# A Restormer block on one core: a table moves single instructions along their engines, and a second replay hands out the buffers

## The chip, the cores and the metric

The kernel runs on one core of a Trainium2 chip. The metric is device time in microseconds of that core, from three runs of the kernel before: 3977.29, 3972.34 and 3972.2 us, median 3972.34 us. Shares and waits come from one profiled execution; a line number such as L1185 is a line of the kernel before, and in the changed kernel the same line of the function stands 590 lines further down (L1775).

## The reference

One transformer block over x of 16 x 128 x 96 x 96 (images, channels, rows, columns), all in fp32:

```
xn1 = layernorm(x over channels)
x   = x + attention(xn1)        # channel attention: 8 heads of 16 channels,
                                # q and k normalised over all 9216 pixels, softmax of a 16x16 matrix per head
xn2 = layernorm(x over channels)
h1  = w_in (512 x 128) @ xn2    # 1x1 convolution
h2  = depthwise 3x3 convolution of h1 (512 channels, zero padding)
x   = x + w_out (128 x 512) @ gelu(h2)
```

## The kernel before

An image's 96 rows are cut into 8 bands of 12 rows (`BR`), a band into 3 units of 4 rows (`UR`, 384 pixels); channels lie on the 128 partitions. The 512 hidden channels are 4 chunks of 128. Images overlap in time: while the bands of image i run through the convolutions, image i+1 goes through its first layernorm and its Gram matrix.

- **First norm (`norm`, second=False).** TensorE transposes 4 x 128 pixels (L872), ScalarE copies them out of PSUM (zT, L909), VectorE takes statistics (L880), GpSimd makes variance and its power -1/2 (ve_a, L885 and L889) and scales (L913), TensorE adds to the Gram matrix (g, L920) and transposes back (L968), ScalarE places the rows into the ring xn (L974).
- **Attention (`attention`)**, once an image: some 15 dependent steps that go from engine to engine, among them the product a on VectorE (L1112) and the TensorE product that reads it (L1116).
- **Second norm.** Mixing (L822, L831), the addition of x by an accumulating DMA that GpSimd issues (L834), transposes, statistics, variance and power (ve_b), transpose of the scales (L968) and the product into xn (VectorE, L972).
- **Depthwise convolution (`conv_job`)**, 467 jobs of one band and one chunk, spread over four engines. TensorE makes the hidden rows in 3 pieces (L1166), ScalarE copies each out of PSUM (L1171). Of the nine taps ScalarE multiplies two or three (pr, L1182). GpSimd adds the first of them to the middle tap (merged, L1185; at chunk 0 of a band that has a fourth such tap also L1188), and issues two accumulating DMAs: one product is added to another (pr<-pr, L1207), and that sum to the result (h<-pr, L1210). VectorE runs a chain of five taps or so: the **first tap** reads h1 and merged and writes the PSUM tile acc (L1194), middle taps add to acc (L1198), the last tap writes the result h3 (h<-h,ratio,acc, L1194). The second DMA lands on that result, and ScalarE's gelu (L1215) follows it.
- In some bands the fourth chunk's convolution is nine TensorE products (`by_matmuls`, L1278, gelu L1290 and L1292).
- **Output (`ffn_out`).** Four TensorE products per unit (L1314), VectorE adds to x (L1321), SyncE stores (L1325). SyncE also loads x (L799).

TensorE has four PSUM banks (h) for everything but the Gram matrix and acc. There are 8 pr, 8 h3 and 4 zT buffers, 5 and 2 buffers of x.

The order of the work isn't that of the loops. Each step is handed to the class `Plan` by `op` with its engine, a duration in ns, a place, its inputs and outputs; `order` (L283) plays these steps through once by events: when an engine is free it takes the ready step with the lowest place (a position with offsets from AT and SHIFTS). A step that needs a buffer takes one in that play. The order of the starts is the program, and every engine executes its own instructions strictly in that order. The durations are constants: a power on GpSimd 1020 ns (`T_POWER` = 360 + 165 x 4), a variance 190, an accumulating DMA's issue 890, a merge 2400. GpSimd and VectorE have one rule between them there: a GpSimd step that would begin while a first tap runs waits until that tap's end (L346).

```python
            elif engine == "POOL":
                rest = max(0, self.two - time) if k != self.ahead else 0
```

Of the kernel before, what the change touches and what calls it, by code (L numbers as in the profile page):

```python
# [46 lines left out]
ZT_BUFS = 4  # L47
BATCHES = 8
DIRECT = False
IN_TURN = ("zT", "tr", "h3", "pr", "xb", "x1")  # L50
AT = dict(
    load_w=-385.3, weights=-616.15, zeros=-141.7, load_a=-42.4, forth_a=-588.2, stats_a=1671.35, variance_a=269.75,
# [156 lines left out]
    31: dict(merge=3850.3, hidden=-0.2, kept=4295.2, products=1.1, tap=402.3, add_first=4907.6, gelu=-5949.9,  # L209
        conv=-11.3, conv_gelu=3477.9, out=2968.8, add=-5.3, store=-425.9),  # L210
}
STEP = dict(scaled=0.3, hidden=0.1, products=0.5, tap=0.166, conv=1.6, conv_tap=0.03, out=0.8, out_part=0.05)
SLACK = 150
LATE = 400
# [2 lines left out]
WAIT = dict(POOL=1090, SP=1300, ACT=1300)  # L217
# [19 lines left out]
class Plan:  # L237
# [6 lines left out]

    def __init__(self, **pools):
        self.free = {p: list(range(n)) for p, n in pools.items()}
        self.slot = {}
        self.ops, self.writer, self.readers, self.users = [], {}, {}, {}
        self.dma = 0.0
        self.two = self.held = self.lost = self.pool_free = 0.0  # L250
        self.ahead = None
# [31 lines left out]
    def order(self):  # L283
        ops, free = self.ops, self.free
# [5 lines left out]
        held = [[] for _ in ops]  # L290
        pending = {}
# [12 lines left out]
        events, starts, count = [], [None] * len(ops), 0  # L304
# [17 lines left out]
        def dispatch(engine, time):  # L322
# [13 lines left out]
            for t in o[5]:  # L336
                self.slot[t] = free[t[0]].pop(0)
                if t[0] in IN_TURN:
                    turn[t[0]].pop()
# [34 lines left out]
        while events:  # L374
            time, _, kind, what = heapq.heappop(events)
# [18 lines left out]
            if idle[what]:  # L394
                dispatch(what, time)
        assert None not in starts, "the buffers do not suffice"
        self.end = max(starts)
        return [ops[k][3] for k in sorted(range(len(ops)), key=lambda k: (starts[k], k))]


@with_exitstack
def tile_restormer_block(
# [175 lines left out]
    def t_dve(n):  # L578
        return 100 + 1.067 * n if n > 2 * UT else 67 + 1.05 * n
# [223 lines left out]
    def norm(i, second, place_of):  # L803
# [44 lines left out]
        def pixels(s, m):  # L848
# [11 lines left out]
            apart = i == 0 and not second  # L860
            from_psum = second or DIRECT or apart

# [90 lines left out]
        def zt_of(q):  # L953
            return ("h3", ("zT", q // 2), q % 2) if i == 0 and not second else ("zT", (name, q))
# [192 lines left out]
    def conv_job(j, g, n):  # L1147
# [115 lines left out]
    def by_matmuls(p, g, s):  # L1263
# [135 lines left out]
```

## Time and profile before

| | |
|---|---|
| time, median of 3 runs | 3972.34 us |
| profiled execution: span from the first to the last instruction | 3968.9 us |
| its time as a run | not listed; the median is 3.4 us above the span |
| busy: TensorE, VectorE, ScalarE, GpSimd | 3849.0, 3832.0, 3605.0, 3390.7 us |
| TensorE weight loads | 2482.4 us |
| DMA | 777.38 MB, mean 196 GB/s |
| granted TensorE clock | 0.997 |

Busy is the time in which an engine has an instruction under way, so the rest of the span is what it waited or had no work. TensorE and VectorE are both busy for 97% of the span; no single engine is the bound by a clear distance. What can change without any instruction changing is the idle time, and the views that show it are the busy time by stretches (500 us each, the columns are PE, PEld, DVE, ACT, POOL busy), the waits (engine, tile and line that waited, what ended the wait, us in total, times, longest) and the timeline (start, duration, engine, line, operation). PE is TensorE, DVE VectorE, ACT ScalarE, POOL GpSimd, SP SyncE.

### The profile page before, as it was taken

To read this page: it belongs to the slowest core of one execution; us is meant where nothing else is said; L and a number is where in the kernel's file an instruction comes from. 1 tells how busy PE (TensorE), PEld (TensorE's weight loads), DVE (VectorE), ACT (ScalarE), POOL (GpSimd) and SP (SyncE) were. 2 spreads that over 40 slices of the span, in tenths; PEclk is the share of its full clock that TensorE was granted. 3 is DMA by queue.
4 is the path that set the end of the run, shared out by engine and by line. 5 is a ranking of instruction groups with operands and counts; after the bars stand their busy time and mean duration, and the time that the engine had idled before them with its cause. 6 is when DMAs were issued, how large, how long until landed. Compare 5 with 4: busy or idle time off the path is not lost.

```text
span 3968.9 us, 50596 instructions
## 1 busy us (share of the span) xinstructions
PE 3849.0 (97%) x16467; PEld 2482.4 (63%) x16467; DVE 3832.0 (97%) x4392; ACT 3605.0 (91%) x5478; POOL 3390.7 (85%) x3107
## 2 busy tenths in 40 slices
PE   8999999999999999999999999999999999999999
PEld 7566666666666666666666666666666666666555
DVE  7999999999999999999999999999999999999998
ACT  3999899999899998999999999999999999999986
POOL 5998988888798898998889898888998888888674
PEclk9999999999999999999999999999999999999999
DMA  3999899999899999999999999999999999999996
GB/s 99 186 201 207 190 201 200 192 206 194 192 202 199 199 198 202 199 201 212 198 202 200 206 204 200 210 191 211 200 197 198 207 211 191 201 205 188 200 189 146
DMA packets 191689, 777.38 MB, mean 196 GB/s; under 512 B 22208, under 2 KB 23616, under 8 KB 191424
## 3 DMA queue, kind: packets, MB, share of 16 engines
q0 software_dynamic: 151920, 622.33, 82.7%
q1 hardware_dynamic: 38784, 151.75, 10.3%
q8 instruction: 129, 2.11, 0.2%
q14 instruction: 136, 1.11, 0.1%
q10 hardware_dynamic: 720, 0.07, 0.0%
HBM read 148.85 MB, written 75.50 MB: 57 GB/s over the span
## 4 chain that ended last, share of the span: by engine, by line
PE 24%; DVE 10%; ACT 5%; POOL 4%; DMA 4%; issue 3%; DVEq 0%; POOLq 0%; ACTq 0%
PE h L1314 7%; PE h L1166 6%; PE h L1278 6%; DVE acc L1198 5%; ACT pr L1182 2%; DMA pr<-pr 2%; DVE acc L1194 2%; DVE h L1194 2%; DMA h<-pr 2%; PE h L822 2%; PE h L968 1%; POOL merged L1185 1%; PE h L872 1%; PE g L920 1%; POOL merged L1188 1%
## 5 line engine op out<-in xcount | busy, mean ns | idle before, releaser
L1182 ACT ACTIVATE pr<-h,ratio 128x1152 f32<-128x1152 f32 x1494 | 1841.2, 1275 | 37.3 <-DMA pr<-pr 10.1
L1198 DVE SCALAR_TENSOR_TENSOR acc<-h,ratio,acc 128x1152 f32<-128x1152 f32 (+1 forms) x1308 | 1809.4, 1383 | 8.4
L1185 POOL TENSOR_TENSOR merged<-pr,h 128x1152 f32<-128x1152 f32 x466 | 1239.9, 2661 | 102.2 <-DVE acc L1194 48.5
L1166 PE MATMUL h<-xn,winT 128*128 128x384 f32 (+2 forms) x2802 | 1082.9, 495 | 17.8 <-ACT h L1171 6.1
L1314 PE MATMUL h<-h,woutT 128*128 128x384 f32 x3072 | 1079.4, 487 | 6.2 <-ACT h L1171 3.2
L1278 PE MATMUL h<-xn,comp 128*128 128x380 f32 (+2 forms) x2430 | 894.7, 483 | 7.6 <-ACT h L1171 4.0
L1314 PEld LDWEIGHTS h<-h,woutT 128*128 128x128 f32 x3072 | 567.9, 190 | 379.4 <-ACT h L1171 14.3
L1171 ACT COPY h<-h 128x384 f32<-128x384 f32 (+2 forms) x1401 | 653.2, 498 | 140.6 <-PE h L1166 137.4
L1194 DVE SCALAR_TENSOR_TENSOR acc<-h,ratio,merged 128x1152 f32<-128x1152 f32 x466 | 683.9, 1468 | 33.8 <-POOL merged L1188 13.9
L1166 PEld LDWEIGHTS h<-xn,winT 128*128 128x128 f32 x2802 | 499.0, 190 | 343.1 <-issue 34.9
L1210 POOL DMA_DIRECT2D h<-pr x466 | 476.2, 1022 | 236.6 <-DVE h L1194 54.6
L1215 ACT ACTIVATE h<-h,ksum 128x1152 f32<-128x1152 f32 (+1 forms) x586 | 616.9, 1085 | 53.7 <-DMA h<-pr 49.5
L1194 DVE SCALAR_TENSOR_TENSOR h<-h,ratio,acc 128x1152 f32<-128x1152 f32 x467 | 654.8, 1402 | 3.5
L1278 PEld LDWEIGHTS h<-xn,comp 128*128 128x128 f32 x2430 | 429.9, 190 | 237.9 <-issue 16.7
L1207 POOL DMA_DIRECT2D pr<-pr x466 | 487.4, 1059 | 73.8 <-ACT pr L1182 55.0
L889 POOL TENSOR_TENSOR ve_b<-ve_b,mhalf 128x4 f32<-128x4 f32 x288 | 377.8, 1325 | 7.9
L889 POOL TENSOR_TENSOR ve_a<-ve_a,mhalf 128x4 f32<-128x4 f32 x288 | 349.2, 1214 | 10.9
L913 POOL TENSOR_TENSOR zT<-zT,ve_a 128x512 f32<-128x512 f32 x270 | 348.2, 1295 | 6.4
L872 PE MATMUL h<-ident,x 128*128 128x128 f32 x2244 | 317.4, 275 | 18.3 <-ACT xn L974 4.6
L872 PEld LDWEIGHTS h<-ident,x 128*128 128x128 f32 x2244 | 262.3, 141 | 110.2 <-issue 37.9
L822 PE MATMUL h<-xn,mwT 128*128 128x384 f32 x768 | 289.9, 493 | 11.4 <-ACT x L831 6.5
L920 PEld LDWEIGHTS g<-zT 128*128 128x128 f32 x2160 | 270.2, 191 | 39.0 <-POOL zT L913 6.9
(187 smaller groups left out, 3923.2 us busy)
## 6 DMA issues: line engine op xcount, KB each, us to landing
pr<-pr POOLq DMA_DIRECT2D x466, 576.0 KB, 8.0
h<-pr POOLq DMA_DIRECT2D x466, 576.0 KB, 7.9
x<-in_x_dram SPq DMA_DIRECT2D x128, 576.0 KB, 7.5
out_dram<-x SPq DMA_DIRECT2D x127, 576.0 KB, 4.9
x<-in_x_dram POOLq DMA_DIRECT2D x123, 576.0 KB, 9.5
out_dram<-x SPq DMA_DIRECT2D x3, 192.0 KB, 1.9
h<-in_L_conv_w_in_dram SPq DMA_DIRECT2D x1, 256.0 KB, 4.4
h<-in_L_conv_w_out_dram SPq DMA_DIRECT2D x1, 256.0 KB, 4.5
```

Source lines behind the costliest of these rows:

```text
L872: nc.tensor.transpose(d["pT", q][:, k, :], xt[:, j * P : (j + 1) * P], ident)
L889: nc.gpsimd.tensor_tensor(rstd, rstd, mhalf, ALU.pow)
L1166: nc.tensor.matmul(rows(ph), lhsT=winT[:, n, :], rhs=window(xn, r0 + r, e - r, 1), start=True, stop=True)
L1171: nc.scalar.copy(window(h1_, r, e - r, 1), rows(d.pop(("ph", r))))
L1182: nc.scalar.activation(to, shifted(t), AF.Copy, scale=ratio[:, n, t : t + 1])
L1185: nc.gpsimd.tensor_tensor(merged, d["pr", dma_taps[0]], shifted(UNIT), ALU.add)
L1194: nc.vector.scalar_tensor_tensor(to, shifted(t), ratio[:, n, t : t + 1], also, ALU.mult, ALU.add)
L1198: nc.vector.scalar_tensor_tensor(to, shifted(t)[:, lo:hi, cut], ratio[:, n, t : t + 1], to, ALU.mult, ALU.add)
L1207: nc.gpsimd.dma_start(out=d["pr", dma_taps[1]], in_=d["pr", t], accum_op=ALU.add)
L1215: nc.scalar.activation(h3, h3, AF.Gelu, bias=ksum[:, z, n : n + 1])
L1278: nc.tensor.matmul(d["pc"][:, lo:hi, cut], lhsT=comp[:, t, :], rhs=window(xn, r0 + dy, UR, dx)[:, lo:hi, cut], start=(t == order[0]), stop ...
L1314: nc.tensor.matmul(rows(d["po"]), lhsT=woutT[:, n, :], rhs=h3s[g, n][:, s * UR : (s + 1) * UR, :], start=(k == 0), stop=(k == NCH - 1),)
```

## The change

No step, duration or place is altered, and both programs hold the same 10556 matmuls (as the program counts them), 4391 VectorE, 5451 ScalarE (and 32 table loads), 3103 GpSimd instructions and 264 SyncE DMAs. What is new comes after the play by events: its starts give a list of steps for each engine (and for each buffer pool that more than one engine takes from). `MOVES` then takes single steps out of such a list and puts them back some positions earlier (negative) or later: 1348 entries for PE, 790 for DVE, 2024 for ACT, 1050 for POOL, 13 for SP (all of them earlier, by 1 to 5), 27 for the pools h and h3. A second replay, `in_turn`, plays the moved lists strictly in order, and its choice of buffers and sequence is the program. Its waits are more detailed: a GpSimd DMA issue begins 480 ns after the end of a VectorE step that it needs, 240 after a ScalarE step; and a GpSimd step that is already running when a first tap begins ends 126 ns after that tap.

```diff
+MOVES = dict(
+    PE={6: -1, 11: -1, 13: -1, 18: 0, 19: -3, 26: -1, 28: -1, 29: 7, 33: -3, 37: 3, 38: 6, 39: -4, 47: -2, 48: -2,
...
+)
+ISSUE, FROM_POOL, PORT = dict(DMA=500, DVE=480, ACT=240), 170, 126
+PE_RATE, SPARE = 0.989, 75
...
-        return [ops[k][3] for k in sorted(range(len(ops)), key=lambda k: (starts[k], k))]
+        lists = {e: [] for e in ENGINES}
...
+        lists.update({p: ks for p, ks in takes.items() if len(takers[p]) > 1})
+        for name, ks in lists.items():
+            lists[name] = moved(ks, MOVES.get(name, {}))
+        return [ops[k][3] for k in self.in_turn(lists)]
...
+                if engine == "POOL" and ops[k][8]:
+                    from_ += ISSUE["DMA"] if ops[d][8] else ISSUE.get(of, 0)
+                elif of == "POOL" and engine == "DVE" and not ops[d][8]:
+                    from_ += FROM_POOL
...
+                    time = max(times[e], port) if ops[k][9] and last_two != e else times[e]
+                    if e == "POOL" and not ops[k][8]:
+                        time = max(time, taken)
...
+                if engine == "DVE":
+                    taken, at = time + ns, free_at["POOL"]
+                    if last_pool is not None and not ops[last_pool][9] and time < at < taken + PORT:
+                        by = taken + PORT - at
+                        free_at["POOL"] += by
...
+def moved(ks, moves):
+    rest = [k for n, k in enumerate(ks) if n not in moves]
+    for n, by in sorted(moves.items(), key=lambda m: m[0] + m[1]):
+        rest.insert(n + by, ks[n])
+    return rest
```

Three places show what the moves are like; the prediction calls them A, B and C.

**Place A, GpSimd, image 8, band 5 (about 2212 to 2218 us of the profile).** Before, the merge for chunk 2 (L1185 reading h_2) stands behind the variance and power of group 15, the addition of x, an accumulating DMA and the variance of group 16:

```order
L885 TENSOR_SCALAR ve_b_15_14692<-st_b_15_14667 128x4
L834 DMA x_9_0_14654<-in_x_dram 128x1152
L1207 DMA pr_148<-pr_145 128x1152
L889 TENSOR_TENSOR ve_b_15_14692<-ve_b_15_14692,mhalf 128x4
L885 TENSOR_SCALAR ve_b_16_14712<-st_b_16_14695 128x4
L1185 TENSOR_TENSOR merged<-pr_146,h_2_142 128x1152
L889 TENSOR_TENSOR ve_b_16_14712<-ve_b_16_14712,mhalf 128x4
```

and in the changed kernel (the numbers in the names are buffers, and differ):

```order
L1475 TENSOR_SCALAR ve_b_15_14667<-st_b_15_14648 128x4
L1775 TENSOR_TENSOR merged<-pr_147,h_2_142 128x1152
L1479 TENSOR_TENSOR ve_b_15_14667<-ve_b_15_14667,mhalf 128x4
L1800 DMA h_7_160<-pr_148 128x1152
L1475 TENSOR_SCALAR ve_b_17_14707<-st_b_17_14696 128x4
L1475 TENSOR_SCALAR ve_a_4_14711<-st_a_4_14673 128x4
```

The merge is now right behind the variance of group 15; the power of group 15 and the accumulating DMA into h3 (L1800, before L1210) stand behind it.

**Place B, TensorE, the attention of image 6 (about 1495 to 1506 us).** g is the attention's PSUM tile, L1099 its transpose, L1116 the product that reads a; the others are output products (L1314), transposes of the next image (L872), convolution products (L1278) and hidden rows (L1166). Before:

```order
L1099 MATMUL g_8324<-ident,kq_9968 128x128
L1314 MATMUL h_74<-h_4_157,woutT 128x384
L1314 MATMUL h_75<-h_1_154,woutT 128x384
L872 MATMUL h_76<-ident,x_0_9449 128x128
L872 MATMUL h_76<-ident,x_1_9941 128x128 x3
L1314 MATMUL h_75<-h_2_155,woutT 128x384
L1314 MATMUL h_75<-h_7_160,woutT 128x384
L872 MATMUL h_74<-ident,x_1_9941 128x128 x4
L1314 MATMUL h_75<-h_4_157,woutT 128x384
L1278 MATMUL h_73<-xn,comp 128x384
L1278 MATMUL h_73<-xn,comp 128x4x95
L1314 MATMUL h_76<-h_1_154,woutT 128x384
```

after which comes L1116. The changed kernel has, again from the transpose (now L1689) to the row ahead of the product (L1706):

```order
L1689 MATMUL g_8386<-ident,kq_9970 128x128
L1462 MATMUL h_73<-ident,x_0_9451 128x128
L1462 MATMUL h_73<-ident,x_1_9944 128x128 x3
L1868 MATMUL h_74<-xn,comp 128x4x95 x2
L1868 MATMUL h_74<-xn,comp 128x384
L1904 MATMUL h_75<-h_6_159,woutT 128x384
L1462 MATMUL h_76<-ident,x_1_9944 128x128 x4
L1868 MATMUL h_74<-xn,comp 128x4x95
L1904 MATMUL h_73<-h_1_154,woutT 128x384
L1756 MATMUL h_76<-xn,winT 128x384
L1904 MATMUL h_73<-h_4_157,woutT 128x384
L1756 MATMUL h_75<-xn,winT 128x384
```

Besides the same eight transposes, nine products stand between the two instead of eight, and two of them are hidden rows (L1756, before L1166) that stood behind L1116.

**Place C, GpSimd, image 4, band 6, chunk 0 (about 1250 to 1259 us).** Here the first tap waits for two merges in a row, L1185 and L1188. Before:

```order
L885 TENSOR_SCALAR ve_a_2_8429<-st_a_2_8417 128x4
L1185 TENSOR_TENSOR merged<-pr_148,h_0_140 128x1152
L889 TENSOR_TENSOR ve_a_2_8429<-ve_a_2_8429,mhalf 128x4
L1210 DMA h_2_155<-pr_151 128x1152
L913 TENSOR_TENSOR zT_164<-zT_164,ve_a_2_8429 128x4x128
L1188 TENSOR_TENSOR merged<-merged,pr_146 128x1152
```

and in the changed kernel:

```order
L1475 TENSOR_SCALAR ve_a_2_8418<-st_a_2_8392 128x4
L1424 DMA x_5_0_8349<-in_x_dram 128x1152
L1479 TENSOR_TENSOR ve_a_2_8418<-ve_a_2_8418,mhalf 128x4
L1775 TENSOR_TENSOR merged<-pr_147,h_0_140 128x1152
L1503 TENSOR_TENSOR zT_164<-zT_164,ve_a_2_8418 128x4x128
L1800 DMA h_4_157<-pr_148 128x1152
L1778 TENSOR_TENSOR merged<-merged,pr_151 128x1152
```

The power of that group (L1479) has gone ahead of the first merge, and the addition of x (L1424) has come down to stand ahead of it; two steps instead of three lie between the merges.

More of the change, by code (lines that the diff above doesn't have):

```diff
@@ L49 @@
 DIRECT = False
+ENGINES = ("PE", "DVE", "ACT", "POOL", "SP")
 IN_TURN = ("zT", "tr", "h3", "pr", "xb", "x1")
@@ L211 @@
 }
+MOVES = dict(
+    PE={6: -1, 11: -1, 13: -1, 18: 0, 19: -3, 26: -1, 28: -1, 29: 7, 33: -3, 37: 3, 38: 6, 39: -4, 47: -2, 48: -2,
[122 rows of a table added]
+    DVE={2: -1, 8: 0, 9: -2, 12: -1, 16: -1, 18: -1, 19: 2, 24: -2, 32: 0, 37: -6, 39: -1, 40: -4, 42: 0, 43: -3,
[70 rows of a table added]
+    ACT={5: -1, 7: -1, 10: -1, 22: 2, 26: 2, 43: 5, 46: 1, 49: 5, 53: -3, 62: -3, 63: 4, 66: -2, 67: 3, 68: -7,
[180 rows of a table added]
+    POOL={0: 5, 2: 4, 4: 5, 5: 18, 6: 5, 7: 19, 18: -3, 21: -3, 28: -1, 30: -2, 32: -1, 37: 4, 39: 4, 42: -3, 44: -4,
[92 rows of a table added]
+    SP={8: -5, 17: -1, 36: -1, 52: -1, 71: -1, 73: -1, 80: -1, 103: -1, 116: -1, 119: -1, 186: -1, 224: -1,
+        231: -1},
+    h={24: -1, 1596: -1, 3091: -1},
+    h3={0: 3, 15: -1, 26: -1, 38: -2, 73: -1, 85: -1, 96: -1, 134: -1, 158: -1, 193: -1, 218: -1, 231: -3, 241: -1,
+        278: -1, 313: -1, 327: -1, 337: -2, 349: -1, 361: -1, 386: -1, 469: -1, 492: -1, 502: -1, 519: 2},
+)
+ISSUE, FROM_POOL, PORT = dict(DMA=500, DVE=480, ACT=240), 170, 126
+PE_RATE, SPARE = 0.989, 75
 STEP = dict(scaled=0.3, hidden=0.1, products=0.5, tap=0.166, conv=1.6, conv_tap=0.03, out=0.8, out_part=0.05)
@@ L246, in __init__ @@
         self.free = {p: list(range(n)) for p, n in pools.items()}
+        self.slots = dict(pools)
         self.slot = {}
@@ L396, in order @@
         assert None not in starts, "the buffers do not suffice"
-        self.end = max(starts)
-        return [ops[k][3] for k in sorted(range(len(ops)), key=lambda k: (starts[k], k))]
+        lists = {e: [] for e in ENGINES}
+        takes, takers = {p: [] for p in free}, {p: set() for p in free}
+        for k in sorted(range(len(ops)), key=lambda k: (starts[k], k)):
+            lists[ops[k][0]].append(k)
+            for p in {t[0]: None for t in ops[k][5]}:
+                takes[p].append(k)
+                takers[p].add(ops[k][0])
```

79 lines of the change are left out of this document (added), and 464 rows, old and new, of tables (ACT, DVE, PE, POOL).

## The prediction

> **What bounds the kernel now.** First the page's head: two engines are busy for 97% of the span, so nothing but idle time is to be won, and on both.
>
> ```profile
> span 3968.9 us, 50596 instructions
> ...
> PE 3849.0 (97%) x16467; PEld 2482.4 (63%) x16467; DVE 3832.0 (97%) x4392; ACT 3605.0 (91%) x5478; POOL 3390.7 (85%) x3107
> ```
>
> Next the busy time by stretches (stretch, its length, busy us of PE, PEld, DVE, ACT, POOL with their instructions, clock, DMA share, GB/s), which tells where the idle time lies.
>
> ```profile
> 0.00:20.00 20.00, 12.68 (x77) 11.05 (x78) 10.20 (x26) 1.48 (x2) 10.72 (x46) 1.00 0.77 247
> ...
> 100.00:500.00 400.00, 381.50 (x1663) 248.10 (x1661) 388.27 (x441) 373.16 (x565) 357.88 (x323) 1.00 0.94 196
> 500.00:1000.00 500.00, 487.31 (x2067) 312.77 (x2067) 485.07 (x547) 461.58 (x700) 435.83 (x393) 1.00 0.95 200
> 1000.00:1500.00 500.00, 480.24 (x2048) 309.44 (x2048) 479.15 (x542) 460.57 (x699) 431.31 (x392) 0.99 0.94 196
> 1500.00:2000.00 500.00, 490.05 (x2115) 317.69 (x2114) 494.50 (x557) 465.81 (x712) 443.66 (x404) 1.00 0.96 202
> 2000.00:2500.00 500.00, 488.86 (x2106) 314.05 (x2106) 488.09 (x559) 468.13 (x711) 443.98 (x403) 1.00 0.97 204
> 2500.00:3000.00 500.00, 489.68 (x2116) 316.34 (x2115) 488.47 (x554) 468.17 (x708) 442.18 (x402) 1.00 0.96 203
> 3000.00:3500.00 500.00, 486.49 (x2085) 313.65 (x2084) 489.69 (x555) 468.75 (x713) 440.15 (x402) 1.00 0.96 202
> 3500.00:3900.00 400.00, 389.89 (x1481) 239.40 (x1480) 393.31 (x415) 366.10 (x544) 319.65 (x269) 1.00 0.95 192
> 3900.00:3920.00 20.00, 20.00 (x68) 11.87 (x67) 18.91 (x16) 18.58 (x27) 13.33 (x10) 1.00 0.98 203
> 3920.00:3940.00 20.00, 20.00 (x65) 11.95 (x64) 16.82 (x16) 11.60 (x17) 6.40 (x6) 1.00 0.78 164
> ```
>
> From 100 to 3900 us TensorE is idle for 18.50 + 12.69 + 19.76 + 9.95 + 11.14 + 10.32 + 13.51 + 10.11 = 106.0 us, VectorE for 11.73 + 14.93 + 20.85 + 5.50 + 11.91 + 11.53 + 10.31 + 6.69 = 93.5. Within 500 us TensorE's idle time goes from 9.95 to 19.76 and VectorE's from 5.50 to 20.85, though every stretch does nearly the same work: luck in the order makes up a factor of two or more. At the very end TensorE has no gap at all while VectorE already has, so TensorE paces the end, and a gain must come from TensorE too.
>
> Then the waits: who waits for whom, us, times, longest.
>
> ```profile
> DVE x L1321 <- PE h L1314: 27.1, 31, 3.1
> DVE acc L1194 <- POOL merged L1188: 13.9, 17, 2.5
> ...
> ACT h L1171 <- PE h L1166: 137.4, 176, 4.7
> ACT h L1215 <- DMA h<-pr: 49.5, 43, 6.1
> ...
> PE g L1116 <- DVE a L1112: 8.8, 4, 4.1
> PE h L968 <- POOL ve_b L889: 8.1, 10, 2.5
> ...
> PE acc L872 <- DMA x<-in_x_dram: 5.5, 1, 5.5
> ```
>
> No wait is large. On the two full engines each is about 1 us, scattered over all pairs, with GpSimd on the releasing side in several: that is the shape of an order laid out on durations that the chip doesn't quite keep.
>
> **The change, part by part.** Nothing is added or removed, so the durations stay and each term is a wait. The first question is whether the order before was laid out on wrong durations. The groups (busy, mean ns of one, idle before) say so for GpSimd:
>
> ```profile
> L1194 DVE SCALAR_TENSOR_TENSOR acc<-h,ratio,merged 128x1152 f32<-128x1152 f32 x466 | 683.9, 1468 | 33.8 <-POOL merged L1188 13.9 <-POOL merged L1185 11.3 <-POOL ve_b L889 0.5
> L1194 DVE SCALAR_TENSOR_TENSOR h<-h,ratio,acc 128x1152 f32<-128x1152 f32 x467 | 654.8, 1402 | 3.5
> L1210 POOL DMA_DIRECT2D h<-pr x466 | 476.2, 1022 | 236.6 <-DVE h L1194 54.6 <-PE h L1314 35.7 <-issue 16.5
> L889 POOL TENSOR_TENSOR ve_b<-ve_b,mhalf 128x4 f32<-128x4 f32 x288 | 377.8, 1325 | 7.9
> L885 POOL TENSOR_SCALAR ve_b<-st_b 128x4 f32<-128x4 f32 x288 | 153.9, 547 | 40.0 <-DVE st_b L880 39.6
> ```
>
> A power is planned at 1020 ns and takes 1325 on average, a variance at 190 and takes 547, an issue at 890 and takes 1022: for these three groups 288 x 0.305 + 288 x 0.357 + 466 x 0.132 = 252 us more than planned, part of which the old play books as its rest after a first tap. Why a power is long shows in the timeline, under a first tap and free:
>
> ```profile
> 2008.50 1.40 DVE L1194 SCALAR_TENSOR_TENSOR acc<-h,ratio,merged 128x1152 f32<-128x1152 f32 x1
> 2008.69 2.07 POOL L889 TENSOR_TENSOR ve_b<-ve_b,mhalf 128x4 f32<-128x4 f32 x1
> ...
> 2022.88 1.03 POOL L889 TENSOR_TENSOR ve_a<-ve_a,mhalf 128x4 f32<-128x4 f32 x1
> ```
>
> The power loses about 1.0 us beside the tap. The new replay books this also for a step that was running already, and books the idle time before an issue (the L1210 row: 54.6 us behind VectorE). It lays the moves out on waits that the trace has, which is my reason to expect a gain at all. The three places show its size.
>
> Place A:
>
> ```profile
> 2205.63 2.50 DVE L1194 SCALAR_TENSOR_TENSOR acc<-h,ratio,merged 128x1152 f32<-128x1152 f32 x1
> ...
> 2213.06 1.97 POOL L889 TENSOR_TENSOR ve_b<-ve_b,mhalf 128x4 f32<-128x4 f32 x1
> 2214.26 3.35 POOL L1185 TENSOR_TENSOR merged<-pr,h 128x1152 f32<-128x1152 f32 x1
> ...
> 2217.64 1.43 DVE L1194 SCALAR_TENSOR_TENSOR acc<-h,ratio,merged 128x1152 f32<-128x1152 f32 x1 [1.07 <-POOL merged L1185]
> ```
>
> The tile merged is free from 2208.13 (2205.63 + 2.50), but the merge ends at 2217.61 because GpSimd does other work first; VectorE waits 1.07 us. Moved ahead it ends several us sooner and the 1.07 goes; behind it the power and the DMA into h3 start up to 3.35 us later, which the transpose of the scales (L968) and the gelu (L1215) then feel if they have no slack.
>
> Place B (with ten matmul passes, two to a product, for the pace):
>
> ```profile
> 1499.70 5.48 DVE L1112 TENSOR_SCALAR a<-em,rden 128x128 f32<-128x128 f32 x1
> ...
> 1502.18 2.90 POOL L1188 TENSOR_TENSOR merged<-merged,pr 128x1152 f32<-128x1152 f32 x1
> ...
> 1505.23 0.80 PE L1116 MATMUL g<-wpT,a 128*128 128x128 f32 x2 [4.12 <-DVE a L1112]
> ...
> 1507.35 0.48 ACT L1171 COPY h<-h 128x384 f32<-128x384 f32 x1 [4.68 <-PE h L1166]
> ...
> 2436.84 3.23 PE h L1314 x10
> ```
>
> VectorE's product ends 0.10 us after GpSimd's merge (1505.18 against 1505.08): held for 5.48 us. TensorE, in order, waits 4.12 and ScalarE's copy 4.68 behind it. One product more between L1099 and L1116 covers 2 x 0.323 = 0.65 us of TensorE's 4.12; the hidden rows ahead of L1116 free ScalarE. The cause stays, since the replay lets VectorE wait for GpSimd only at first taps, not at this product.
>
> Place C:
>
> ```profile
> 1250.78 2.44 POOL L1185 TENSOR_TENSOR merged<-pr,h 128x1152 f32<-128x1152 f32 x1 [0.78 <-ACT pr L1182]
> 1253.18 1.02 POOL L889 TENSOR_TENSOR ve_a<-ve_a,mhalf 128x4 f32<-128x4 f32 x1
> ...
> 1258.79 1.43 DVE L1194 SCALAR_TENSOR_TENSOR acc<-h,ratio,merged 128x1152 f32<-128x1152 f32 x1 [2.54 <-POOL merged L1188]
> ```
>
> A power of 1.02 us leaves the path between the two merges and partly fills GpSimd's 0.78 of waiting ahead of the first. The tap's 2.54 falls to about 1.5 if the first merge keeps its time, less if the DMA issue now ahead of it delays it.
>
> So the places save 1.07 of 1.07, 0.65 of 4.12 and 1.0 of 2.54: 2.7 of 7.7 us, about a third, before anything is given back. For the whole I take the state that this kernel already reaches by luck: every stretch like TensorE's best, 9.95 us idle in 500. Over 3800 us that is 75.6, so 106.0 - 75.6 = 30.4 us are saved, 29%; VectorE would keep 93.5 - 30.4 = 63.1, or 8.3 in 500, between its best and its mean. Ends: TensorE's idle halved once more (37.8, a gain of 68) and every stretch like the worst (150.2, a loss of 44).
>
> The other terms I take at nothing. Start: in the first 20 us TensorE is idle for 7.32, of it 5.5 before the first x lands, which no order changes; bound 3 either way. End: TensorE is full, cover and pace at once, and its work is the same; bound 3 either way. First taps held by GpSimd, as at 2205.63 (2.50 against 1.40): (1468 - 1402) x 466 = 31 us in the run; which GpSimd step follows a merge decides it, and in the two orders this is a compute step 253 and 251 times, so no change, bound 31 either way. SyncE's 13 moves bring loads and stores forward by at most five places in a queue with slack; no cost.
>
> The sum: 3972.3 (the span 3968.9 plus the 3.4 us by which the median of the runs stands above it) - 30.4 = 3941.9, say 3942 us.
>
> **The rivals.** *VectorE alone is the bound.* The Trainium skill (Perfetto Trace Analysis, Identifying the Most-Contended Engine) says that TensorE's headroom is not to be judged by its matmul busy time but by its weight loads; these are busy for 63% here, and by that rule VectorE is the one engine to relieve. Then TensorE's gaps only follow VectorE's, and VectorE can come to its own best stretch everywhere: 5.50 x 7.6 = 41.8 us idle, a gain of 51.6, 3921 us. Against it: at 3920 to 3940 TensorE is full and VectorE isn't.
>
> *The waits only change their place.* Every engine stays in order and is coupled to four others; at place B 0.65 of 4.12 goes. What one engine gains stands as idle time at its next partner: 3972 us, within 0.2% (7.9 us, about what a measurement can tell from none).
>
> *Slower: GpSimd's DMA issues come late.* Where a merge is pulled ahead as at A, the issue into h3 moves back by a merge, the DMA lands later, and the gelu holds ScalarE's queue with the PSUM copies (L1171) in it, so that TensorE lacks a bank. Now 43 gelus wait 49.5 us, 1.15 each. If that doubles and all of it passes on to TensorE, the time is 3942 + 49.5 = 3991. It decides from 30.4 / 1.15 = 26 more such waits on. For it: 1050 entries move GpSimd's steps. Against it: ScalarE has 364 us idle, 137.4 of them waiting for TensorE, so half or more of such waits should be swallowed.
>
> That the change does nothing is excluded by the order at the three places.
>
> **How the numbers follow.** Forecast 3942: 0.48 (its own range 3925 to 3958, idle time of TensorE from 59 to 92). VectorE alone, 3921: 0.21. Unchanged, 3972: 0.11. Slower, 3991: 0.20. The two faster cases and a sliver of the slower one's weak end give faster 0.70, same 0.11, slower 0.19. The range: below, it goes past 3921 towards the halved idle time (3972 - 68 = 3904) and ends at 3910, with some 0.07 beyond; above, it ends at 3987, a little short of the slower case, with 0.12 beyond.
>
> **What would show it.** Right: TensorE's idle time between 100 us and the end of the last full stretch at 60 to 90 us, VectorE's at 50 to 75, the waits x <- L1314 and acc <- merged down by a third or more, and the powers' mean below 1325. Wrong: the gelu's wait for its DMA well above 49.5 us with ScalarE's copies behind it (the slower case); VectorE's idle time below 45 while TensorE keeps 90 (VectorE alone); both sums as before on other lines (unchanged). A mean of the first taps far from 1468 would mean that the term I took at nothing decided.

## The result and the profile after

The changed kernel takes 3924.87 us (median of 4 runs, 3919.88 to 3926.66) against 3972.27 us before (median of 4, 3969.53 to 3977.29): a ratio of 0.9878, 95% interval [0.9864, 0.9892], so 47.4 us or 1.2% faster. The forecast was 3942 us with a range of 3910 to 3987. The profiled execution took 3923.85 us, of which the span is 3921.9. One execution of the experiments further down, 4985.0 us of e3 at a granted clock of 0.764, is not counted in any figure here.

The page's head of the changed kernel (busy time, share of the span, instructions):

```profile
span 3921.9 us, 50494 instructions
...
PE 3846.4 (98%) x16467; PEld 2477.5 (63%) x16467; DVE 3824.6 (98%) x4392; ACT 3614.9 (92%) x5478; POOL 3368.7 (86%) x3107
```

The span is 47.0 us shorter. On TensorE that is 44.4 us of idle time (3968.9 - 3849.0 = 119.9 before, 3921.9 - 3846.4 = 75.5 now) and 2.6 us of busy time. Where the idle time went shows in the busy time by stretches of the changed kernel (stretch, its length, busy us of PE, PEld, DVE, ACT, POOL with their instructions, clock, DMA share, GB/s):

```profile
100.00:500.00 400.00, 388.44 (x1682) 250.83 (x1682) 392.05 (x443) 377.10 (x570) 358.31 (x325) 0.99 0.95 198
500.00:1000.00 500.00, 494.10 (x2108) 317.91 (x2107) 494.62 (x561) 472.51 (x716) 440.33 (x401) 1.00 0.97 204
1000.00:1500.00 500.00, 491.48 (x2112) 316.75 (x2111) 491.24 (x552) 474.25 (x726) 438.38 (x403) 1.00 0.97 203
1500.00:2000.00 500.00, 493.61 (x2158) 321.67 (x2156) 495.24 (x566) 472.65 (x713) 450.37 (x409) 1.00 0.98 206
2000.00:2500.00 500.00, 490.46 (x2079) 312.12 (x2078) 491.93 (x557) 468.23 (x708) 440.71 (x402) 1.00 0.97 202
2500.00:3000.00 500.00, 493.70 (x2132) 319.50 (x2131) 493.03 (x564) 476.65 (x722) 445.67 (x406) 1.00 0.97 204
3000.00:3500.00 500.00, 491.01 (x2122) 317.93 (x2121) 492.91 (x559) 473.90 (x718) 441.35 (x405) 1.00 0.97 204
3500.00:3850.00 350.00, 345.30 (x1285) 207.62 (x1284) 346.45 (x363) 324.77 (x477) 273.91 (x235) 1.00 0.96 193
```

TensorE is idle for 11.56 + 5.90 + 8.52 + 6.39 + 9.54 + 6.30 + 8.99 + 4.70 = 61.9 us, VectorE for 52.5. Before it was 106.0 and 93.5 up to 3900 us. TensorE has no gap between 3850 and 3900 there, so its two sums compare; VectorE's sum of before up to 3850 is 92.0. Every full stretch of 500 us now has less than the 9.95 us of idle time that was the best before, and they lie closer together (5.90 to 9.54, against 9.95 to 19.76). The clock is as before. At the start TensorE is busy for 12.61 of the first 20 us against 12.68, and 35.73 of the last 39.3 against 35.75: neither end moved.

The waits of the changed kernel that answer to those shown of before (who waits for whom, us, times, longest; the lines are numbered 590 higher, so L1904 was L1314):

```profile
DVE x L1911 <- PE h L1904: 18.8, 18, 6.3
DVE acc L1784 <- POOL merged L1775: 4.7, 9, 1.4
DVE acc L1784 <- POOL merged L1778: 3.7, 7, 1.2
...
ACT h L1761 <- PE h L1756: 104.3, 181, 2.9
ACT h L1805 <- DMA h<-pr: 26.1, 27, 2.7
```

The first tap's waits for the merges fell from 13.9 + 11.3 to 3.7 + 4.7 us, the gelu's for its DMA from 43 waits of 49.5 us to 27 of 26.1, ScalarE's for the hidden rows from 137.4 to 104.3, TensorE's for the product a from 8.8 to 0.7. No pair of those shown before grew. Others did, such as those of GpSimd, the least busy of the four, for the statistics of the second and the first norm: from 39.6 and 35.1 to 52.1 and 45.9 us. In the groups (busy, mean ns, idle before), the work itself is nearly the same:

```profile
L1784 DVE SCALAR_TENSOR_TENSOR acc<-h,ratio,merged 128x1152 f32<-128x1152 f32 x466 | 678.2, 1455 | 10.6 <-POOL merged L1775 4.7 <-POOL merged L1778 3.7
...
L1479 POOL TENSOR_TENSOR ve_a<-ve_a,mhalf 128x4 f32<-128x4 f32 x288 | 356.7, 1241 | 10.9
L1479 POOL TENSOR_TENSOR ve_b<-ve_b,mhalf 128x4 f32<-128x4 f32 x288 | 339.8, 1195 | 10.0
```

The first tap loses 13 ns of its mean (1468 before). The powers of the second norm fell from 1325 to 1195 ns, but those of the first rose: the same row of before has

```profile
L889 POOL TENSOR_TENSOR ve_a<-ve_a,mhalf 128x4 f32<-128x4 f32 x288 | 349.2, 1214 | 10.9
```

Place A in the changed kernel's timeline (start, us, engine, line, step):

```profile
2176.91 2.44 POOL L1775 TENSOR_TENSOR merged<-pr,h 128x1152 f32<-128x1152 f32 x1
2179.32 1.03 POOL L1479 TENSOR_TENSOR ve_b<-ve_b,mhalf 128x4 f32<-128x4 f32 x1
2182.36 0.92 POOL L1800 DMA_DIRECT2D h<-pr  x1 [2.01 <-PE h L1868]
...
2184.84 1.42 DVE L1784 SCALAR_TENSOR_TENSOR acc<-h,ratio,merged 128x1152 f32<-128x1152 f32 x1
```

The merge ends at 2179.35, 5.5 us ahead of its tap, and the tap waits for nothing; the DMA issue pushed behind it waits 2.01 us for TensorE anyway. Place B:

```profile
1468.94 2.43 POOL L1775 TENSOR_TENSOR merged<-pr,h 128x1152 f32<-128x1152 f32 x1
1471.45 2.73 POOL L1778 TENSOR_TENSOR merged<-merged,pr 128x1152 f32<-128x1152 f32 x1
...
1471.40 0.29 DVE L1702 TENSOR_SCALAR a<-em,rden 128x128 f32<-128x128 f32 x1
...
1474.98 0.27 PE L1706 MATMUL g<-wpT,a 128*128 128x128 f32 x1
```

The product a starts at 1471.40, in the gap between two merges (1471.37 to 1471.45), and takes 0.29 us where it took 5.48; TensorE's 4.12 us of waiting are gone. Place C:

```profile
1230.49 0.56 DVE L1911 TENSOR_TENSOR x<-h,x 128x384 f32<-128x384 f32 x1 [1.38 <-PE h L1904]
1231.86 0.56 DVE L1911 TENSOR_TENSOR x<-h,x 128x384 f32<-128x384 f32 x1 [0.80 <-PE h L1904]
...
1233.74 1.43 DVE L1784 SCALAR_TENSOR_TENSOR acc<-h,ratio,merged 128x1152 f32<-128x1152 f32 x1 [0.65 <-POOL merged L1778]
```

The first tap waits 0.65 us, where it waited 2.54. Just ahead of it VectorE stands 1.38 + 0.80 = 2.18 us for two output products; before, it stood 1.51 us there for one:

```profile
1255.69 0.56 DVE L1321 TENSOR_TENSOR x<-h,x 128x384 f32<-128x384 f32 x1 [1.51 <-PE h L1314]
```

So of the 1.89 us that the tap no longer waits, 0.67 came back ahead of it.

### The profile page after: what moved, and what is told of

Same layout as the page of the kernel before. It is cut to its first block, busy times and chain, and to the rows that moved or that the text cites. A ratio compares the mean times of both kernels' runs of the same rounds, so it can differ in the third digit from the quotient of the medians.

```text
span 3921.9 us, 50494 instructions
## 1 busy us (share of the span) xinstructions
PE 3846.4 (98%) x16467; PEld 2477.5 (63%) x16467; DVE 3824.6 (98%) x4392; ACT 3614.9 (92%) x5478; POOL 3368.7 (86%) x3107
## 4 chain that ended last, share of the span: by engine, by line
PE 40%; DVE 9%; ACT 5%; DMA 3%; issue 2%; POOL 2%; POOLq 0%; DVEq 0%; ACTq 0%
PE h L1904 11%; PE h L1756 10%; PE h L1868 8%; DVE acc L1788 4%; PE h L1412 3%; PE h L1558 3%; PE g L1510 2%; PE h L1462 2%; ACT pr L1772 2%; DMA h<-pr 2%; DVE acc L1784 2%; DVE h L1784 1%; ACT h L1805 1%; DMA pr<-pr 1%; ACT h L1761 1%
## 5 line engine op out<-in xcount | busy, mean ns | idle before, releaser
L1772 ACT ACTIVATE pr<-h,ratio 128x1152 f32<-128x1152 f32 x1494 | 1845.2, 1268 | 14.2 <-DMA pr<-pr 2.7
L1775 POOL TENSOR_TENSOR merged<-pr,h 128x1152 f32<-128x1152 f32 x466 | 1212.6, 2602 | 116.6 <-DVE acc L1784 56.1
L1756 PE MATMUL h<-xn,winT 128*128 128x384 f32 (+2 forms) x2802 | 1093.3, 496 | 17.9 <-ACT h L1761 5.5
L1904 PE MATMUL h<-h,woutT 128*128 128x384 f32 x3072 | 1098.6, 487 | 3.6 <-ACT h L1761 1.4
L1904 PEld LDWEIGHTS h<-h,woutT 128*128 128x128 f32 x3072 | 563.8, 189 | 372.6 <-ACT h L1761 16.4
L1761 ACT COPY h<-h 128x384 f32<-128x384 f32 (+2 forms) x1401 | 654.4, 492 | 110.2 <-PE h L1756 104.3
L1756 PEld LDWEIGHTS h<-xn,winT 128*128 128x128 f32 x2802 | 495.7, 189 | 348.5 <-ACT h L1761 29.7
L1784 DVE SCALAR_TENSOR_TENSOR acc<-h,ratio,merged 128x1152 f32<-128x1152 f32 x466 | 678.2, 1455 | 10.6 <-POOL merged L1775 4.7
L1805 ACT ACTIVATE h<-h,ksum 128x1152 f32<-128x1152 f32 (+1 forms) x586 | 611.0, 1069 | 27.0 <-DMA h<-pr 26.1
L1800 POOL DMA_DIRECT2D h<-pr x466 | 477.1, 1032 | 165.1 <-DVE h L1784 18.5
L1797 POOL DMA_DIRECT2D pr<-pr x466 | 469.6, 1025 | 73.7 <-ACT pr L1772 50.9
L1479 POOL TENSOR_TENSOR ve_a<-ve_a,mhalf 128x4 f32<-128x4 f32 x288 | 356.7, 1241 | 10.9
L1479 POOL TENSOR_TENSOR ve_b<-ve_b,mhalf 128x4 f32<-128x4 f32 x288 | 339.8, 1195 | 10.0
L1503 POOL TENSOR_TENSOR zT<-zT,ve_a 128x512 f32<-128x512 f32 x270 | 339.5, 1260 | 7.0
```

What stands on the lines that cost most here:

```text
L1479: nc.gpsimd.tensor_tensor(rstd, rstd, mhalf, ALU.pow)
L1756: nc.tensor.matmul(rows(ph), lhsT=winT[:, n, :], rhs=window(xn, r0 + r, e - r, 1), start=True, stop=True)
L1761: nc.scalar.copy(window(h1_, r, e - r, 1), rows(d.pop(("ph", r))))
L1772: nc.scalar.activation(to, shifted(t), AF.Copy, scale=ratio[:, n, t : t + 1])
L1775: nc.gpsimd.tensor_tensor(merged, d["pr", dma_taps[0]], shifted(UNIT), ALU.add)
L1784: nc.vector.scalar_tensor_tensor(to, shifted(t), ratio[:, n, t : t + 1], also, ALU.mult, ALU.add)
```

## The experiments

My theory after the result: the gain is the table's, and what counts is that the four engines' lists fit each other, stretch by stretch. The rivals: the buffers of the new replay give part of it; GpSimd's list carries it alone; each engine's moves carry a share; VectorE alone is the bound and the table happened to relieve it.

| kernel | what it is | us, median | ratio to before, interval |
|---|---|---|---|
| e1_replay_only | order of before, buffers by the second replay | 3972.23 | 1.0006 [0.9996, 1.0015] |
| e2_no_hold | order of the change, replay without the hold | 3920.46 | 0.9874 [0.9859, 0.9889] |
| e3_without_pool_moves | all moves but GpSimd's | 4291.89 | 1.0808 [1.079, 1.0827] |
| e4_pool_moves_alone | GpSimd's moves alone | 4239.55 | 1.0675 [1.066, 1.0691] |
| e5_first_half | moves of the front half | 3940.29 | 0.9919 [0.9904, 0.9934] |
| e6_second_half | moves of the back half | 3961.64 | 0.9977 [0.9967, 0.9987] |
| e7_without_vector_moves | all moves but VectorE's | 4203.51 | 1.0582 [1.0566, 1.0597] |
| a1_from_psum | the change, a read from PSUM | 3920.08 | 0.9863 [0.9847, 0.988] |
| l1_vector_lighter | the change, less work on VectorE | 3915.02 | 0.9855 [0.9836, 0.9875] |
| l2_tensor_lighter | the change, less work on TensorE | 3909.87 | 0.9844 [0.9829, 0.9859] |
| l3_both_lighter | both | 3895.64 | 0.9805 [0.979, 0.9819] |
| a2_from_psum_no_hold | a1 and e2 together | 3913.27 | 0.9854 [0.9839, 0.987] |

**e1 and e2: the replay.** e1 applies no move, e2 takes the hold on GpSimd out of the replay. In e2 the order on every engine is that of the changed kernel, and 4365 of 6794 buffers are other ones.

```diff
 e1
-            lists[name] = moved(ks, MOVES.get(name, {}))
+            lists[name] = moved(ks, MOVES.get(name, {}) if name in () else {})
 e2
-                        time = max(time, taken)
+                        pass
-                    if last_pool is not None and not ops[last_pool][9] and time < at < taken + PORT:
+                    if False:
```

> The table is empty, so every engine has the order of the kernel before; only the buffers (PSUM banks, pr buffers) come from the second replay. Buffer theory (a good part of the 47 us comes from which bank or buffer a step gets, since a bank that came free earlier is taken first): 3930 to 3955 us. Order theory (the gain is in the moves alone): 3964 to 3980 us, TensorE's idle time between 100 and 3850 us still near 105 us.

> The changed kernel, but its second replay doesn't hold GpSimd back beside a first tap; the moves and so each engine's order are the same, and only the banks and buffers given out differ. If the hold matters through the buffers: 3935 us or more. Order theory: within 0.2% of the changed kernel, 3917 to 3933 us.

e1 is the kernel before within 0.15%, and TensorE's idle time between 100 and 3850 us is 112.3 us in its profiled execution (the slowest of its ten, 3981.25 us). e2 is within the interval of the changed kernel. So the buffers give nothing that can be measured, nor does the hold through them: the 47 us come from the order, that is from the table.

**e3, e4 and e7: the moves of some engines alone.** A part of the table leaves orders that block each other at some points; there the first later step that doesn't block is taken (against the lists of before, e3 has 12 GpSimd steps at another place by that, e7 53 VectorE steps, e4 about 40 steps on the other engines).

```diff
 e3 (e4 and e7 alike, with their own names)
-            lists[name] = moved(ks, MOVES.get(name, {}))
+            lists[name] = moved(ks, MOVES.get(name, {}) if name in ('PE', 'DVE', 'ACT', 'SP', 'h', 'h3') else {})
```

> All moves except GpSimd's, whose steps keep the order of before (twelve of them change place, where the order would block itself). GpSimd theory (what the new order knows is GpSimd's true durations, so its list carries the gain): at least 30 of the 47 us are lost, 3955 us or more. Spread theory (every engine's moves remove their own waits): a quarter to a third is lost, 3935 to 3945 us. Matching theory (the lists fit only each other, and a foreign list is worse than none): slower than before, 3980 us or more.

> Only GpSimd's moves; the other engines keep the order of before but for some forty steps where it would block itself. GpSimd theory: 3925 to 3945 us. Spread theory: about 3960 us. Matching theory: 3980 us or more.

> All moves except VectorE's, whose list changes least (1704 of 4292 steps stand at another place, against 3532 of 6261 on TensorE). Matching theory (the lists of the engines fit each other only as a set): slower than before as in the two runs on GpSimd's list, though less so, 4020 to 4250. Rival (each engine's moves carry a share of the gain): 3930 to 3955.

All three are far slower than before, by 322, 270 and 232 us. The page's head of e3:

```profile
PE 3955.4 (92%) x16467; PEld 2514.9 (59%) x16467; DVE 3862.9 (90%) x4392; ACT 3629.7 (85%) x5478; POOL 3415.1 (80%) x3107
```

Not all of the loss is idle time of TensorE. Its busy time is 3955.4, 3938.1 and 3933.0 us in e3, e4 and e7 against 3849.0 before, with a granted clock of 0.977, 0.980 and 0.987 against 0.997; that is about a third of the 321, 274 and 228 us by which the spans are longer. The rest is waiting. What they wait for, first of e3 (lines 18 higher than in the changed kernel where they are behind the replay):

```profile
POOL pr L1815 <- ACT pr L1790: 274.6, 99, 10.1
...
PE h L1576 <- POOL ve_b L1497: 111.3, 62, 6.5
ACT h L1823 <- DMA h<-pr: 102.2, 44, 5.8
```

and of e7:

```profile
POOL ve_a L1493 <- DVE st_a L1488: 180.2, 78, 12.7
```

With GpSimd's old list, GpSimd stands at a DMA issue up to 10.1 us for a product of ScalarE, whose list is the new one (274.6 us in all, 55.0 before); behind it in its queue are the powers, and TensorE waits for these. With VectorE's old list, GpSimd stands up to 12.7 us for VectorE's statistics (180.2 us in all, 35.1 before). An engine in order at the wrong step holds everything behind it. So neither does GpSimd's list carry the gain, nor do the gains of the engines add: the moves of one engine taken away, or put in alone, cost about five to seven times what the whole gives. That VectorE's list has the fewest moves (1704 of 4292 steps at another place) doesn't save e7. The steps that had to be displaced may be some of the cost; they are 12, some 40 and 53 against waits by the hundred, but their share wasn't measured by itself.

**e5 and e6: the front and the back half.** The cut is where the lists of before and after hold the same steps ahead of it, so no step is displaced: each kernel has the order of one ahead of the cut and that of the other behind it.

```diff
+CUT = {'PE': 3093, 'DVE': 2160, 'ACT': 2473, 'POOL': 1573, 'SP': 136, 'h': 1835, 'h3': 256}
-            lists[name] = moved(ks, MOVES.get(name, {}))
+            lists[name] = moved(ks, (lambda m: {n: b for n, b in m.items() if n < CUT.get(name, 0)})(MOVES.get(name, {})))
```

> Only the moves of the front half of each engine's list are made (TensorE's up to step 3093, VectorE's up to 2160, ScalarE's up to 2473, GpSimd's up to 1573; about the first 2000 us); behind the cut the lists are those of before. Local theory (each stretch gains by its own moves, whatever the lists do a thousand us later): TensorE's idle time fell from 60.9 to 32.4 us between 100 and 2000 us and from 45.1 to 29.5 us behind it, so this kernel gains 28 of the 47 us: 3940 to 3948. Rival (the lists fit only as a whole, so a cut in the middle costs what a foreign list costs): at or above 3972.

> The other half: only the moves behind the cut. Local theory: a gain of 16 to 19 us, 3951 to 3957, and the gains of the two halves add up to that of the whole table (47 us) within 6 us. Rival (the lists fit only as a whole): at or above 3972; or the gain sits in the front alone: 3970 to 3975.

The gains are 31.4 and 10.0 us (against 3971.67 for the kernel before, measured beside them), together 41.4 of 47.4; the front as expected, the back below its 16 to 19. That leaves 6.0 us missing, just at the limit that was set for the two halves to add up. The trace shows the locality better than the times do. The two stretches on either side of the cut, in the order before, after, e5, e6:

```profile
100.00:2000.00 1900.00, 1839.11 (x7889) 1188.00 (x7888) 1846.99 (x2084) 1761.11 (x2672) 1668.68 (x1509) 0.99 0.95 199
2000.00:3850.00 1850.00, 1804.91 (x7608) 1153.11 (x7608) 1811.04 (x2030) 1726.03 (x2609) 1606.54 (x1440) 1.00 0.96 201
```

```profile
100.00:2000.00 1900.00, 1867.62 (x8057) 1207.17 (x8056) 1873.15 (x2119) 1796.51 (x2721) 1687.39 (x1535) 1.00 0.97 203
2000.00:3850.00 1850.00, 1820.46 (x7614) 1157.17 (x7613) 1824.32 (x2040) 1743.56 (x2623) 1601.64 (x1444) 1.00 0.97 201
```

```profile
100.00:2000.00 1900.00, 1867.97 (x8063) 1208.44 (x8062) 1872.66 (x2120) 1798.69 (x2723) 1689.21 (x1538) 1.00 0.97 203
2000.00:3850.00 1850.00, 1804.19 (x7557) 1150.03 (x7556) 1808.33 (x2025) 1721.27 (x2601) 1596.28 (x1431) 1.00 0.96 200
```

```profile
100.00:2000.00 1900.00, 1833.73 (x7844) 1182.34 (x7842) 1840.21 (x2075) 1754.40 (x2659) 1661.07 (x1501) 1.00 0.95 198
2000.00:3850.00 1850.00, 1817.81 (x7655) 1157.33 (x7654) 1823.44 (x2039) 1741.85 (x2625) 1604.92 (x1449) 1.00 0.97 202
```

TensorE's idle time in front of 2000 us is 60.9 before, 32.4 after, 32.0 in e5 and 66.3 in e6; behind it 45.1, 29.5, 45.8 and 32.2. Each half has, to within 5.4 us, the idle time of the order that it runs, whatever the other half does. (The profiled execution of e6 was the slowest of its nine, 3968.16 us.) So the table works across the engines, but along the time only locally.

**l1, l2 and l3: which engine sets the pace.** The order is that of the changed kernel; the work of one engine, or of both, is cut.

```diff
 l1
+            hi -= j % 2
             to = acc[:, lo:hi, cut]
 l2
-                rows(d["po"]), lhsT=woutT[:, n, :], rhs=h3s[g, n][:, s * UR : (s + 1) * UR, :],
+                rows(d["po"])[:, : UR - (k == 1 and g % 5 > 0), :], lhsT=woutT[:, n, :],
+                rhs=h3s[g, n][:, s * UR : (s + 1) * UR - (k == 1 and g % 5 > 0), :],
```

> The changed kernel, same order, with VectorE's middle taps one row of 12 shorter in every second job (part of the convolution is left out): about 1810 x 1/24 = 75 us less work on VectorE, TensorE's work as it was. If VectorE alone is the bound and TensorE's gaps only follow it: 30 to 55 us faster than the changed kernel, 3870 to 3895 (TensorE's 3846 us of work and its start set the floor). If TensorE paces: within 8 us of 3925. If the two are bound by the waits between them: 10 to 25 us faster.

> The changed kernel, same order, with one of the four output products a row of 4 shorter in four bands of five (part of the last sum is left out): about 768 x 0.8 x 0.122 = 75 us less work on TensorE, VectorE's as it was. If TensorE paces: 30 to 55 us faster, 3870 to 3895 (VectorE's 3825 us, its start of 28 and its tail set the floor). If VectorE alone is the bound, as the rule that judges TensorE by its weight loads (63% busy) has it: within 8 us of 3925. If both: 10 to 25 us faster.

> Both edits at once: about 75 us less work on each of the two full engines. If one engine alone is the bound: as the better of the two single runs. If both are: 55 to 75 us faster than the changed kernel, 3850 to 3870, and clearly more than the two single gains together.

The pages' heads of l1, l2 and l3:

```profile
PE 3839.3 (98%) x16467; PEld 2478.0 (63%) x16467; DVE 3772.4 (96%) x4392; ACT 3613.7 (92%) x5478; POOL 3383.4 (86%) x3107
```

```profile
PE 3815.6 (98%) x16467; PEld 2470.7 (63%) x16467; DVE 3818.4 (98%) x4392; ACT 3611.7 (92%) x5478; POOL 3362.3 (86%) x3107
```

```profile
PE 3808.5 (98%) x16467; PEld 2476.5 (64%) x16467; DVE 3766.5 (97%) x4392; ACT 3608.4 (93%) x5478; POOL 3378.0 (87%) x3107
```

The edits took less busy time than I had reckoned: 3824.6 - 3772.4 = 52.2 us from VectorE, 3846.4 - 3815.6 = 30.8 us from TensorE. Against the changed kernel's 3924.87 us the runs are 9.9, 15.0 and 29.2 us faster; the interval of l1 overlaps that of the changed kernel, those of l2 and l3 don't. So 52 us less on VectorE return about a fifth, 31 us less on TensorE about a half. The intervals of l1 and l2 overlap too, so the two gains aren't told apart as such; for each microsecond of work taken away TensorE's is the larger. It is so on top of the other edit as well: from l1 to l3 TensorE's 30.8 us (3839.3 - 3808.5) bring 19.4, from l2 to l3 VectorE's 51.9 (3818.4 - 3766.5) bring 14.2, and l3's interval lies below those of l1 and l2. That points to TensorE as the nearer bound, with VectorE close behind. l1 falls between the two ranges set for it (within 8 us, or 10 to 25), l2 within the 10 to 25 of two engines bound by the waits between them. l3 missed its 55 to 75, and at 29.2 it isn't clearly above the 24.9 of the two together; but its edits took only 3846.4 - 3808.5 = 37.9 us from TensorE, so three quarters of what TensorE lost came back, more than in l2, where VectorE kept its work. What the rest turns into shows best in l1. Between 100 and 3850 us VectorE's idle time is 52.5 in the changed kernel and

```profile
100.00:3850.00 3750.00, 3690.14 (x15686) 2370.89 (x15685) 3653.02 (x4165) 3543.38 (x5349) 3309.01 (x2984) 1.00 0.97 203
```

3750 - 3653.02 = 97.0 us in l1: 44.5 of the 52.2 us that were taken away came back as waiting. This order, written out for certain durations, gives little back when one of them is shortened.

The Trainium skill (Perfetto Trace Analysis, Identifying the Most-Contended Engine) judges TensorE's room by its share of peak work and by its weight loads; by the latter, 63% here, VectorE would be relieved first. These runs don't bear that out for this kernel: at 63 to 64%, the edit on TensorE returned more from fewer microseconds, alone and on top of the other.

**a1 and a2: the product that GpSimd holds.** In the changed kernel 5 of the 16 executions of the step a are still above 0.5 us. The longest is at another image:

```profile
2160.96 3.56 DVE L1702 TENSOR_SCALAR a<-em,rden 128x128 f32<-128x128 f32 x1
...
2160.85 0.91 POOL L1800 DMA_DIRECT2D h<-pr  x1
2161.54 2.89 POOL L1778 TENSOR_TENSOR merged<-merged,pr 128x1152 f32<-128x1152 f32 x1
```

It ends at 2164.52, 0.09 us behind GpSimd's merge (2164.43). a1 computes the same value from PSUM and the block mask:

```diff
-            nc.vector.tensor_scalar(sb([P, P], "a"), em, v["rden"], None, ALU.mult)
+            nc.vector.scalar_tensor_tensor(sb([P, P], "a"), v["ps_e"], v["rden"], blocks, ALU.mult, ALU.mult)
```

> The changed kernel with the step that makes a (16 times, mean 0.70 us, median 0.29, the longest 3.57 us, 5.48 before) written in a form that reads PSUM, the block mask and the reciprocal as a scalar. If the long ones are VectorE being kept waiting by GpSimd's back-to-back work beside that form, the mean falls to about 0.3 us, the longest below 1 us, and the time by 2 to 6 us: 3918 to 3923. If the long ones are no property of that form, or TensorE and ScalarE stand off them: 3921 to 3928 with a mean that stays above 0.5 us.

The step's durations in a1 (min/median/max, first and last start):

```profile
L1702 DVE SCALAR_TENSOR_TENSOR a<-g,rden,blocks x15: 350/350/354, 238.4 to 3602.9; 128x128 f32<-128x128 f32 x15
```

and in the changed kernel:

```profile
L1702 DVE TENSOR_SCALAR a<-em,rden x16: 285/289/3565, 59.4 to 3604.3; 128x128 f32<-128x128 f32 x16
```

All are 0.35 us (so is the sixteenth, whose PSUM tile has another name), 0.06 more than the median of the old form, and none is long. The same place in a1's timeline shows it under the same neighbours:

```profile
2162.59 0.35 DVE L1702 SCALAR_TENSOR_TENSOR a<-g,rden,blocks 128x128 f32<-128x128 f32 x1
...
2162.49 0.90 POOL L1800 DMA_DIRECT2D h<-pr  x1
2163.18 2.89 POOL L1778 TENSOR_TENSOR merged<-merged,pr 128x1152 f32<-128x1152 f32 x1
```

In both kernels a DMA issue starts 0.1 us ahead of the step and the merge 0.6 us behind its start. In 0.29 us the old form would have been done ahead of the merge, so it was already held under the issue; what holds it there is not shown.

One place could be chance, but the other profiles say the same. The step has 16 executions in each kernel. In the twelve kernels with the old form (before, the changed kernel, e1 to e7, l1 to l3) the longest takes between 2.37 us (e7) and 5.55 us (e6); in the two with the new form, a1 and a2, all 32 take 349 to 354 ns. So the long ones are a property of the form. The Trainium skill (GPSIMD Engine Reference, Specifications) says that GpSimd's SBUF interfaces are shared with VectorE, with contention for VectorE's instructions in a 2-port mode or with two SBUF inputs; the new form has one SBUF tensor input, and its 354 ns at most agree. The old form has only one as well, so by that rule it can contend through the 2-port mode alone; it took up to 3565 ns here, but no run shows the mode. In time, 3920.08 us is in the range expected for this case, but its interval overlaps that of the changed kernel, so the gain isn't settled; 11.2 - 16 x 0.35 = 5.6 us less work on an engine that returns a fifth would be worth about 1 us.

> The two edits that came out lowest, together: the step a in the form that reads PSUM, and the buffers of the replay without the hold. If the 5 us of each are real and independent: 3914 to 3918. If they are the spread of one kernel under different buffers: 3918 to 3926.

With the replay of e2 it is the fastest kernel that computes everything, 3913.27 us, 1.5% below before and just below the 3914 to 3918 expected for two real and independent gains. Against the changed kernel that is 0.24% by the ratios, and the intervals still overlap ([0.9839, 0.987] and [0.9864, 0.9892]): probably better, not shown.

## Why the prediction was right, and where not

- **The signs set beforehand.** TensorE's idle time came to 61.9 us (60 to 90 was named), VectorE's to 52.5 (50 to 75), the first taps' waits for the merges fell by two thirds (25.2 to 8.4), and the powers' mean from 1325 to 1195 ns. VectorE's wait for the output products fell by 31%, just short of the third.
- **The bound.** "A gain must come from TensorE too" held. Of the 47.0 us of span, 44.1 are TensorE's idle time between 100 and 3850 us, 2.6 its busy time and 0.3 the start. l2 against l1 points the same way.
- **The term that was mis-sized** is the sum over the whole: "every stretch like TensorE's best, 9.95 us idle in 500". It gave 75.6 us of idle time and a gain of 30.4; measured were 61.9 and 44.1. The best stretch of before was no floor: all six full stretches came out below it. I had no reason for that floor except that the kernel had reached it once; what was measured lies between it and the halved idle time that I took as the end of the range (14 us below 75.6, 24 above 37.8).
- **The places** gave more than I had added up. A saved its 1.07 as worked out. At B I counted 0.65 of 4.12 by TensorE's cover, and all 4.12 went, since the step a fell into a gap between two merges; "the cause stays" was right (3.56 us at 2160.96, and it goes in a1). Where it strikes goes with the order: the longest is 5.48 us before and 5.53 in e1, which has the same order, 3.57 in the changed kernel and 3.56 in e2. The new replay doesn't book this wait, as I had written, so as far as the prediction goes it is luck that the new order is struck less. At C the tap's wait fell by 1.89 instead of about 1.0, of which 0.67 came back at the output products. Together 6.4 of 7.7 us at the three places, instead of a third; the whole kernel gave 42% (44.1 of 106.0). Three places picked for their waits are no sample.
- **The reason** I gave, that the old order was laid out on durations which the chip doesn't keep, is not shown. The powers of one norm became shorter (1325 to 1195 ns), those of the other longer (1214 to 1241). I also wrote that the replay lays the moves out; it doesn't, the table is fixed and the replay only plays it, and booking the hold in that play gives nothing (e2). What the runs show is that the table as a whole fits the chip better, across all engines and in each stretch by itself (e3 to e7). On what durations it was made, they can't tell.
- **The terms taken at nothing.** Start and end: 0.1 us or less each in the first 20 and the last 39 us, 0.3 up to 100 us. First taps: (1468 - 1455) x 466 = 6 us less on VectorE, against a bound of 31; by l1's fifth that is worth about 1 us.
- **VectorE alone, 3921 us.** The time came nearly there, the mechanism didn't: VectorE's idle time fell to 52.5 us and not to 41.8, and l1 returns a fifth.
- **The waits only change their place.** Not for the table, which lowers the sums on both engines, though 0.67 us did so at place C. l1 shows this mechanism at full size: 44.5 of 52.2 us.
- **GpSimd's DMA issues come late.** The gelu's waits fell to 27 of 26.1 us instead of doubling. At A the issue moved back behind the merge, as I feared, and stood there for TensorE anyway. e3 has the mechanism (102.2 us for the gelu, 111.3 for TensorE's wait on the powers), so it was a real danger: of a list that doesn't fit, not of this one.

## What to carry to other kernels

Where two in-order engines are full to 97% and no wait is large, as here, what is left to tune is the order itself. The moves on one engine cost time in this kernel without their counterparts on the others, and the halves in time kept their own gains: judge such a table whole or by stretches of time, not by engine. Cutting work on one full engine returned a fifth or a half of it here, with the order left as it was. And an estimate by "as good as the best stretch so far" was no floor here: all six full stretches came out below it.

## What the runs showed of the hardware

A matmul pass with 288 columns took 408 ns on average against 489 for one with 384 in l2: a quarter fewer columns for a sixth less time. By these means the 612 shorter passes give 612 x 0.081 = 50 us. The busy time fell by only 30.8 us, 50 ns a pass, as passes in a row overlap (ten take 3.23 us at place B, 323 ns each).

```profile
L1904 PE MATMUL h<-h,woutT 128*128 128x384 f32 x2460 | 922.9, 489 | 4.3 <-ACT h L1761 1.7 <-DVE xn L1562 1.6 <-DVE st_b L1470 0.6
...
L1904 PE MATMUL h<-h,woutT 128*128 128x288 f32 x612 | 199.2, 408 | 0.0
```

A VectorE step of 0.29 us can take 2.4 to 5.5 us beside GpSimd's work where a form that reads PSUM, of 0.35 us, never took more than 354 ns (32 executions in a1 and a2).

The granted TensorE clock went down where TensorE waited more: 0.977 in e3, whose TensorE is busy for 92% of the span, against 0.997 before and 0.999 in the changed kernel, at 97% and 98%.
